# Attention scores and weighted values in two halves each, q's projection as a block of its own, and masks of 32 rows, in a six-layer windowed-attention kernel

## The chip, the core and the metric

The kernel runs on one core of one Trainium2 chip. The metric is device time in microseconds (us) for one execution of the whole program, and of several runs the median. The profile is that of one further execution, so its numbers add up to that execution's own time.

## The reference, cut to what matters

The input has 8 sequences of 512 tokens with 128 features. A first block of attention without a softmax (`_L0_attn_ref`) is followed by six layers of windowed attention and feed-forward. The change concerns the six layers' attention alone. Cut down, with 16 heads of 64 features and windows of 32 tokens, it is:

```python
def attn_layer(x, Wqkv, qs, ksc, Wo):
    q, k, v = jnp.split(x @ Wqkv, 3, -1)          # then split into 16 heads of 64
    q = l2norm(q) * qs;  k = l2norm(k) * ksc      # unit length, scales
    q = q * cos * scale + rotate_half(q) * sin * scale
    k = k * cos / scale + rotate_half(k) * sin / scale
    ...
    # each window of 32 queries sees the window before it and its own: 64 keys
    mask = (it < jb) | (it > jb + w) | (jb == -1)
    sim = jnp.where(mask, -big, jnp.einsum('bhwie,bhwje->bhwij', bq, bk2) * 8.0)
    out = jnp.einsum('bhwij,bhwje->bhwie', softmax(sim), bv2)
    return out @ Wo

for i in range(6):
    x = attn_layer(shift_tokens(x), ...) + x
    x = ffn_layer(shift_tokens(x), ...) + x       # layer norm, 128 -> 2 x 341, gelu, 341 -> 128
```

All of it is in fp32.

## The kernel before, in words

**Units.** The first attention block takes the first part of the program (its lines are L187 to L366). Then comes one long loop over `t` (L703). A *unit* is one layer, one sequence and one block of 128 tokens: 6 x 8 x 4 = 192 units. The loop is a software pipeline, written by hand: in slot `t` the helper `at(t, lag, step)` calls each step for unit `t - lag`, so that a unit is projected in slot `t`, transposed and scored in the next, weighted in the one after, and so on.

**The order of work.** PE's order is the order of the source, since the loop stands in `manual_schedule(engines={PE})` (L694). The order on the other engines is made by a scheduler at build time from priorities; `tc.high_priority()` lifts the copies out of PSUM. Once built, every engine's order is fixed, and engines wait for each other by semaphores.

**A slot before the change**, in PE's order: q's projection (`proj`, L421: 2 products of 512 columns, each of which is 2 MATMUL records[...]), the out-projection of unit t-3 (L603), k's projection, the transposes of the exponentials of unit t-2 (`by_keys`), v's projection (`values`, L481), eight transposes of q and k of unit t-1 (`by_features(0)`: heads 0 to 7, four for q, four for k), the weighted values of unit t-2 (`weigh_values`, L574: 64 small products, 128 MATMUL records), eight more transposes (`by_features(4)`), a piece of the feed-forward part, the mask (L527) and scores (L534, again 128 records) of unit t-1, and eight transposes of unit t-2's result (`out_by_features`). All transposes have the helper's line, L70.

The feed-forward part is spread over four slots, so that each slot holds one piece of it: normalization (transposes into `nx`), transposes of the normalized values (`xn`), three pairs of products with a gelu (L625, L626, L628; these slots also switch ACT's function table and back), and the last product (L657).

**What follows on the other engines.** ACT copies each group of four transposes out of PSUM (L514 for qT and kT, L564 for pT, L596 for oT), squares q and k out of PSUM (L444), copies v (L482), and takes 16 exponentials per unit (L546), which need the maximum that DVE takes over all scores (L542). DVE multiplies q and k by the rotary tables (L429, L436) and divides the weighted values (L582). POOL adds the rotary parts and scales to unit length (L454, L470). SP issues the DMAs that lay v out by windows (L489 to L492).

**PSUM**[...] the ring `mm` (2 buffers of 2 banks: q, k, v and feed-forward products), the ring `tr` (2 buffers of 1 bank: every group of four transposes and the out-projection) and `s` (1 buffer of 2 banks: the scores and, in turn, the weighted values). A group of transposes can start when the group before the last has been copied out; v's projection can start when q's PSUM buffer has been read by DVE and ACT.

**The mask** is added by PE: an identity of 128 rows times the mask, once for each half of the heads, into the bank in which the scores then accumulate.

Of the kernel before, what the change touches and what calls it, by code (L numbers as in the profile page):

```python
# [8 lines left out]
F32 = mybir.dt.float32  # L9
BF16 = mybir.dt.bfloat16  # L10
# [16 lines left out]
def sandwich_kernel(ctx: ExitStack, tc: tile.TileContext, ins: dict, out: bass.AP):  # L27
# [37 lines left out]

    mask = const.tile([P, 2 * W], BF16, tag="mask", name="mask")
    mask0 = const.tile([P, 2 * W], BF16, tag="mask0", name="mask0")

    def transposed(ps, src, rows, cols):
        nc.tensor.transpose(ps[:cols, :rows], src, ident[:rows, :rows])  # L70
# [335 lines left out]

        return dict(wqkv=wqkv, wo=wo, w1=w1, w2=w2, tab=tab)

    def proj(u, s):

        L, b, j = u["L"], u["b"], u["j"]
        wqkv, tab = L["wqkv"], L["tab"]
        lhs = state[b][:, j * P : (j + 1) * P]
        if s == 0:
            u["ss"] = f2.tile([P, 2, H], F32, tag="ss", name="ss")
            u["qk"] = f2.tile([P, 2, H, 2, HF], F32, tag="qk", name="qk")
        ss, qk = u["ss"], u["qk"]

        ps = psum.tile([P, 2, H, HF], F32, tag="mm", name="mm")
        for a in range(2):  # L420
            nc.tensor.matmul(  # L421
                ps[:, a].rearrange("p h d -> p (h d)"), lhs, wqkv[:, s, a, :], start=True, stop=True
            )
        sq = f2.tile([P, H, 2, HF], F32, tag="sq", name="sq")
        t1 = f2.tile([P, 2, H, HF], F32, tag="t1", name="t1")
        t2 = f2.tile([P, 2, H, HF], F32, tag="t2", name="t2")

        def turned(a):
            nc.vector.tensor_tensor(  # L429
                t2[:, a], ps[:, 1 - a],  # L430
                tab[:, 2 * s + 1, j, HF * a : HF * (a + 1)].unsqueeze(1).to_broadcast([P, H, HF]),
                ALU.mult,
            )

        def straight():
            nc.vector.tensor_tensor(  # L436
                t1, ps,
                tab[:, 2 * s, j, :].rearrange("p (a d) -> p a d", a=2).unsqueeze(2)
                .to_broadcast([P, 2, H, HF]),
                ALU.mult,  # L440
            )

        def squared(a):
            nc.scalar.activation(sq[:, :, a, :], ps[:, a], AF.Square)  # L444

        turned(0)
        turned(1)
        straight()
        squared(0)
        squared(1)  # L450
        u["sq"] = sq
        if s == 0:
            sum_squares(u, 0)
        nc.gpsimd.tensor_tensor(qk[:, s].rearrange("p h a d -> p a h d"), t1, t2, ALU.add)  # L454
# [17 lines left out]
            )  # L472

    def values(u):
        L, b, j = u["L"], u["b"], u["j"]
        lhs = state[b][:, j * P : (j + 1) * P]

        v0 = f3.tile([P, 2, 512], F32, tag="v0", name="v0")
        ps = psum.tile([P, 2, 512], F32, tag="mm", name="mm")
        for p in range(2):  # L480
            nc.tensor.matmul(ps[:, p, :], lhs, L["wqkv"][:, 2, p, :], start=True, stop=True)  # L481
        nc.scalar.copy(v0, ps)  # L482

        v2 = f2.tile([P, 4, 512], F32, tag="v2", name="v2")
        for p in range(2):
            if j == 0:
                nc.gpsimd.memset(v2[HD * p : HD * p + W, 0, :], 0.0)
            else:
                nc.sync.dma_start(v2[HD * p : HD * p + W, 0, :], u["B"]["v0"][P - W : P, p, :])  # L489
            nc.sync.dma_start(v2[HD * p + W : HD * (p + 1), 0, :], v0[0:W, p, :])  # L490
            for w in range(1, 4):
                nc.sync.dma_start(  # L492
                    v2[HD * p : HD * (p + 1), w, :], v0[W * (w - 1) : W * (w + 1), p, :]
                )
        u["B"]["v0"] = v0
        u["v2"] = v2

    def by_features(u, c):

        j, qk, B_ = u["j"], u["qk"], u["B"]  # L500
        if c == 0:
            u["qT"] = f1.tile([P, NP, P], F32, tag="qT", name="qT")
            if j == 0:
                B_["kT"] = f2.tile([P, NP, W + P], F32, tag="kT", name="kT")
                nc.gpsimd.memset(B_["kT"][:, :, :W], 0.0)
            u["kT"] = B_["kT"]
        for s in range(2):
            ps = psum.tile([P, 4, P], F32, tag="tr", name="tr")
            for i in range(4):
                h0 = 2 * (c + i)  # L510
                transposed(ps[:, i, :], qk[:, s, h0 : h0 + 2].rearrange("p h a d -> p (h a d)"), P, P)
            dst = u["qT"][:, c : c + 4, :] if s == 0 else u["kT"][:, c : c + 4, W:]
            with tc.high_priority():
                nc.scalar.copy(dst, ps)  # L514
        if c == NP - 4 and j < NB - 1:
            B_["kT"] = f2.tile([P, NP, W + P], F32, tag="kT", name="kT")
            nc.gpsimd.tensor_copy(B_["kT"][:, :, :W], u["kT"][:, :, P:])

    def scores(u):

        qT, kT = u["qT"], u["kT"]


        mk = mask0 if u["j"] == 0 else mask
        sp = psum.tile([P, 2, NP, 2 * W], F32, tag="s", name="sp", bufs=1)
        for p in range(2):
            nc.tensor.matmul(  # L527
                sp[:, p], identb, mk.unsqueeze(1).to_broadcast([P, NP, 2 * W]),
                start=True, stop=False, skip_group_check=True,
            )  # L530
        for pair in range(NP):
            for w in range(4):
                for p in range(2):
                    nc.tensor.matmul(  # L534
                        sp[W * w : W * (w + 1), p, pair, :],
                        qT[HD * p : HD * (p + 1), pair, W * w : W * (w + 1)],
                        kT[HD * p : HD * (p + 1), pair, W * w : W * (w + 2)],
                        start=False, stop=True, skip_group_check=True,
                    )
        mx = f2.tile([P, 2, NP], F32, tag="mx", name="mx")  # L540
        with tc.high_priority():
            nc.vector.tensor_reduce(mx, sp, AX.X, ALU.max, negate=True)  # L542
        pe = f2.tile([P, NP, 2, 2 * W], F32, tag="pe", name="pe")
        for pair in range(NP):
            for p in range(2):
                ex = nc.scalar.activation(  # L546
                    pe[:, pair, p, :], sp[:, p, pair, :], AF.Exp, bias=mx[:, p, pair : pair + 1]
                )
# [14 lines left out]
            with tc.high_priority():  # L563
                nc.scalar.copy(pT[:, c : c + 4, :], ps)  # L564

    def weigh_values(u):

        v2, pT, su = u["v2"], u["pT"], u["su"]
        po = psum.tile([P, 2, NP, HD], F32, tag="s", name="po", bufs=1)
        for pair in range(NP):  # L570
            for w in range(4):
                for p in range(2):
                    r = slice(HD * p, HD * (p + 1))
                    nc.tensor.matmul(  # L574
                        po[W * w : W * (w + 1), p, pair, :],
                        pT[r, pair, W * w : W * (w + 1)],
                        v2[r, w, HD * pair : HD * (pair + 1)],
                        start=True, stop=True,
                    )
        u["on"] = on = f1.tile([P, NP, 2, HD], F32, tag="on", name="on")  # L580
        with tc.high_priority():
            dv = nc.vector.tensor_tensor(  # L582
                on.rearrange("t c p d -> t p c d"), po,
                su.rearrange("t c p -> t p c").unsqueeze(3).to_broadcast([P, 2, NP, HD]), ALU.mult,
            )
        divisions.append(dv)
# [107 lines left out]
    with tc.manual_schedule(engines={mybir.EngineType.PE}):  # L694
# [8 lines left out]
        for t in range(len(units) + 7):  # L703
# [7 lines left out]
            gelus = 0 <= t - 5 < len(units) and units[t - 5]["j"] == NB - 1  # L711
            if gelus:
                gelu_only()
            at(t, 0, proj, 0)
            at(t, 3, out_project)
            at(t, 0, proj, 1)
            at(t, 2, by_keys)

            if t == 0:
                head_norm(NG - 1)  # L720
            at(t, 0, values)
            if t == 1:
                attn_out(B - 1)
            if t == 3:
                to_state(B - 1)
            at(t, 1, by_features, 0)
            at(t, 2, weigh_values)
            at(t, 0, sum_squares, 1)
            if not gelus:
                at(t, 0, unit_length)  # L730
            at(t, 1, by_features, 4)
            at(t, 3, feed_norm, ends=True)
            at(t, 4, feed_first, ends=True)
            at(t, 5, feed_middle, ends=True)
            if gelus:
                at(t, 0, unit_length)
            at(t, 6, feed_last, ends=True)
            at(t, 1, scores)
            at(t, 2, out_by_features)


def _rotary(n):
# [88 lines left out]
```

## Time and profile before

| what | us |
|---|---|
| runs: median of 3 (lowest, highest) | 3899.76 (3896.29, 3900.25) |
| the profiled execution, its own time | 3893.85 |
| span of its profile, first to last instruction | 3892.1 |
| PE busy (matmuls) | 3729.8 |
| DVE busy | 2818.2 |
| ACT busy | 2657.5 |
| POOL busy | 1837.0 |
| matmuls of q's and k's projection, L421 | 727.1 |
| matmuls of v's projection, L481 | 367.9 |
| matmuls of the scores, L534, and of the masks, L527 | 312.2 and 114.6 |
| matmuls of the weighted values, L574 | 299.3 |
| 16 exponentials per unit on ACT, L546 | 651.4 |

How to read the profile: a row of the timeline gives the start (us from the span's start), the time taken, the engine, the line, the operation, the tile written and the tiles read, the shapes, and the number of like instructions merged into the row. In brackets behind it stands the time for which the engine was idle before it, and what ended that idle time. "PEld" rows are weight loads, which overlap the matmuls. In the groups, the first number behind the bar is the busy time (overlaps counted once), the second the mean time of one instruction in ns. Matmuls are pipelined, so that one in a dense run lasts longer than the distance to the next. The granted TensorE clock was 0.99 of full speed.

### The profile page before, as it was taken

To read this page: it belongs to the slowest core of one execution; us is meant where nothing else is said; L and a number is where in the kernel's file an instruction comes from. 1 tells how busy PE (TensorE), PEld (TensorE's weight loads), DVE (VectorE), ACT (ScalarE), POOL (GpSimd) and SP (SyncE) were. 2 spreads that over 40 slices of the span, in tenths; PEclk is the share of its full clock that TensorE was granted. 3 is DMA by queue.
4 is the path that set the end of the run, shared out by engine and by line. 5 is a ranking of instruction groups with operands and counts; after the bars stand their busy time and mean duration, and the time that the engine had idled before them with its cause. 6 is when DMAs were issued, how large, how long until landed. Compare 5 with 4: busy or idle time off the path is not lost.

```text
span 3892.1 us, 149565 instructions
## 1 busy us (share of the span) xinstructions
PE 3729.8 (96%) x65600; PEld 2474.2 (64%) x65600; DVE 2818.2 (72%) x4300; ACT 2657.5 (68%) x6745; POOL 1837.0 (47%) x1311
## 2 busy tenths in 40 slices
PE   8999989999999999999999999999999999999997
PEld 4555456666666666666666666666666666666665
DVE  4555567777867777777777777777787777777775
ACT  5565656776767777777777677777677777766664
POOL 0000025555555555555555555555555555555552
PEclk9999999999999999999999999999999999999998
DMA  2000012222222222222222322223222222222221
GB/s 81 17 9 12 6 50 71 59 66 60 76 74 63 63 63 66 71 75 65 60 62 64 82 65 66 65 56 82 70 66 59 66 65 56 65 68 68 64 67 37
DMA packets 153208, 233.46 MB, mean 60 GB/s; under 512 B 32622, under 2 KB 53356, under 8 KB 151788
## 3 DMA queue, kind: packets, MB, share of 16 engines
q1 hardware_dynamic: 152556, 223.89, 22.4%
q8 instruction: 517, 8.47, 0.9%
q14 instruction: 135, 1.11, 0.1%
HBM read 24.54 MB, written 4.19 MB: 7 GB/s over the span
## 4 chain that ended last, share of the span: by engine, by line
PE 89%; ACT 5%; issue 3%; DVE 2%; DMA 0%; POOL 0%; POOLq 0%; DVEq 0%; SPq 0%; ACTq 0%
PE tr L70 17%; PE mm L421 17%; PE mm L481 9%; PE py L603 9%; PE sp L534 7%; PE po L574 6%; PE y L282 4%; PE mm L625 3%; PE py L657 3%; PE mm L626 3%; PE sc L252 2%; PE sp L527 2%; ACT sq L444 2%; PE vv L230 2%; PE po L318 2%
## 5 line engine op out<-in xcount | busy, mean ns | idle before, releaser
L454 POOL TENSOR_TENSOR qk<-t,t 128x1024 f32<-128x1024 f32 x384 | 909.2, 2368 | 999.6 <-DVE t L436 999.5
L421 PE MATMUL mm<-wqkv,state 128*128 128x512 f32 x1536 | 727.1, 596 | 3.7 <-ACT v L482 2.6
L470 POOL TENSOR_TENSOR qk<-qk,ss 128x1024 f32<-128x1024 f32 x384 | 722.3, 1902 | 16.0
L429 DVE TENSOR_TENSOR t<-mm,tab 128x512 f32<-128x512 f32 x768 | 497.8, 685 | 242.8 <-PE mm L421 231.3
L546 ACT ACTIVATE pe<-sp,mx 128x64 f32<-128x64 f32 x3072 | 651.4, 376 | 27.6 <-DVE mx L542 27.3
L436 DVE TENSOR_TENSOR t<-mm,tab 128x1024 f32<-128x1024 f32 x384 | 465.9, 1213 | 0.0
L457 DVE TENSOR_REDUCE ss<-sq 128x16 f32<-128x1024 f32 x384 | 461.9, 1203 | 2.0 <-ACT sq L444 2.0
L444 ACT ACTIVATE sq<-mm 128x512 f32<-128x512 f32 x768 | 422.6, 610 | 47.2 <-DVE t L436 45.6
L603 PEld LDWEIGHTS py<-oT,wo 128*128 128x128 f32 x3072 | 374.8, 193 | 93.5 <-issue 56.2
L70 PEld LDWEIGHTS tr<-ident,qk 128*128 128x128 f32 x3072 | 345.7, 141 | 127.1 <-issue 105.7
L70 PE MATMUL tr<-ident,qk 128*128 128x128 f32 x3072 | 412.1, 277 | 7.4 <-ACT qT L514 2.3
L596 ACT COPY oT<-tr 128x512 f32<-128x512 f32 x384 | 207.3, 589 | 266.2 <-PE tr L70 265.2
L421 PEld LDWEIGHTS mm<-wqkv,state 128*128 128x128 f32 x1536 | 264.1, 192 | 191.6 <-issue 188.0
L481 PE MATMUL mm<-wqkv,state 128*128 128x512 f32 x768 | 367.9, 602 | 16.8 <-ACT sq L444 16.8
L603 PE MATMUL py<-oT,wo 128*128 128x128 f32 x3072 | 376.0, 276 | 1.0 <-ACT oT L596 0.9
L582 DVE TENSOR_TENSOR on<-po,su 128x1024 f32<-128x1024 f32 x192 | 235.1, 1224 | 170.1 <-PE po L574 170.1
L534 PEld LDWEIGHTS sp<-kT,qT 64*32 64x32 f32 x24576 | 271.9, 106 | 116.7 <-issue 113.8
L574 PE MATMUL po<-v,pT 64*32 64x64 f32 x24576 | 299.3, 225 | 44.7 <-issue 44.7
L482 ACT COPY v<-mm 128x1024 f32<-128x1024 f32 x192 | 194.5, 1013 | 211.0 <-PE mm L481 211.0
L534 PE MATMUL sp<-kT,qT 64*32 64x64 f32 x24576 | 312.2, 227 | 26.0 <-issue 25.2
L574 PEld LDWEIGHTS po<-v,pT 64*32 64x32 f32 x24576 | 258.5, 105 | 86.4 <-issue 86.2
L542 DVE TENSOR_REDUCE mx<-sp 128x16 f32<-128x1024 f32 x192 | 234.6, 1222 | 106.9 <-PE sp L534 106.3
(108 smaller groups left out, 5171.0 us busy)
## 6 DMA issues: line engine op xcount, KB each, us to landing
v<-v SPq DMA_DIRECT2D x1152, 128.0 KB
v<-v SPq DMA_DIRECT2D x672, 64.0 KB
wqkv<-in_L_ffn_Wqkv_dram SPq DMA_DIRECT2D x6, 1536.0 KB
wo<-in_L_ffn_Wo_dram SPq DMA_DIRECT2D x6, 512.0 KB
xin<-_attn_hidden_states_dram SPq DMA_DIRECT2D x8, 256.0 KB
xr<-_attn_hidden_states_dram SPq DMA_DIRECT2D x8, 256.0 KB
x<-xr SPq DMA_DIRECT2D x8, 256.0 KB
xr<-x SPq DMA_DIRECT2D x8, 256.0 KB
```

The source lines that it names most:

```text
L70: nc.tensor.transpose(ps[:cols, :rows], src, ident[:rows, :rows])
L421: nc.tensor.matmul(ps[:, a].rearrange("p h d -> p (h d)"), lhs, wqkv[:, s, a, :], start=True, stop=True)
L429: nc.vector.tensor_tensor(t2[:, a], ps[:, 1 - a], tab[:, 2 * s + 1, j, HF * a : HF * (a + 1)].unsqueeze(1).to_broadcast([P, H, HF]), ALU.mult,
L436: nc.vector.tensor_tensor(t1, ps, tab[:, 2 * s, j, :].rearrange("p (a d) -> p a d", a=2).unsqueeze(2) .to_broadcast([P, 2, H, HF]), ALU.mult,)
L444: nc.scalar.activation(sq[:, :, a, :], ps[:, a], AF.Square)
L454: nc.gpsimd.tensor_tensor(qk[:, s].rearrange("p h a d -> p a h d"), t1, t2, ALU.add)
L470: nc.gpsimd.tensor_tensor(t, t, ss[:, i, :].unsqueeze(2).to_broadcast([P, H, HD]), ALU.mult)
L481: nc.tensor.matmul(ps[:, p, :], lhs, L["wqkv"][:, 2, p, :], start=True, stop=True)
L534: nc.tensor.matmul(sp[W * w : W * (w + 1), p, pair, :], qT[HD * p : HD * (p + 1), pair, W * w : W * (w + 1)], kT[HD * p : HD * (p + 1), pa ...
L546: ex = nc.scalar.activation(pe[:, pair, p, :], sp[:, p, pair, :], AF.Exp, bias=mx[:, p, pair : pair + 1])
L574: nc.tensor.matmul(po[W * w : W * (w + 1), p, pair, :], pT[r, pair, W * w : W * (w + 1)], v2[r, w, HD * pair : HD * (pair + 1)], start=Tru ...
L603: nc.tensor.matmul(py, L["wo"][:, c, :], oT[:, c, :], start=(c == 0), stop=(c == NP - 1))
```

## The change

Six things are changed; the products and sums that are computed stay the same.

1. `proj` is cut into `project(u, s, half)`, one product of 512 columns, and `turn(u, s)`, which holds all that follows q's and k's product on the other engines. v's projection goes through `project` too, and its halves are placed one by one.
2. `weigh_values` runs in two halves of four head pairs each (64 MATMUL records). The first stands between the two halves of v's projection. The division stands on its own (`divide`), behind the second half.
3. `by_features(u, c, s)` makes four transposes at a time, for q (s = 0) or k (s = 1). The first four stand ahead of the second half of the weighted values, and the other twelve behind it.
4. The scores run in two halves. The transposes of `out_by_features` stand between them, and the maximum and exponentials (`softmax`) behind the second half. So the next slot's q projection follows directly on the scores.
5. The mask's left operand is cut to 32 rows: `each` holds four copies of a 32 x 32 identity side by side, on partitions 0 to 31 for the first half of the heads and 32 to 63 for the second. Units with j = 0 (one in four) keep the 128-row identity and `mask0`.
6. `attn_out(B - 1)` of the first attention block moves from slot 1 to the end of slot 0.

The diff, cut to its core:

```diff
+    each = const.tile([2 * W, P], BF16, tag="each", name="each")
+    for a in range(2):
+        for w in range(4):
+            nc.vector.tensor_copy(
+                each[W * a : W * (a + 1), W * w : W * (w + 1)], ident[W * a : W * (a + 1), W * a : W * (a + 1)]
+            )
...
-    def proj(u, s):
+    def project(u, s, half):
+        lhs = state[u["b"]][:, u["j"] * P : (u["j"] + 1) * P]
+        if half == 0:
+            u["proj", s] = psum.tile([P, 2, 512], F32, tag="mm", name="mm")
+        nc.tensor.matmul(
+            u["proj", s][:, half, :], lhs, u["L"]["wqkv"][:, s, half, :], start=True, stop=True
+        )
+    def turn(u, s):
...
-        ps = psum.tile([P, 2, 512], F32, tag="mm", name="mm")
-        for p in range(2):
-            nc.tensor.matmul(ps[:, p, :], lhs, L["wqkv"][:, 2, p, :], start=True, stop=True)
-        nc.scalar.copy(v0, ps)
+        nc.scalar.copy(v0, u.pop(("proj", 2)))
...
-        for s in range(2):
-            ps = psum.tile([P, 4, P], F32, tag="tr", name="tr")
-            for i in range(4):
+        ps = psum.tile([P, 4, P], F32, tag="tr", name="tr")
+        for i in range(4):
...
-    def scores(u):
+    def scores(u, half):
-        mk = mask0 if u["j"] == 0 else mask
-        sp = psum.tile([P, 2, NP, 2 * W], F32, tag="s", name="sp", bufs=1)
-        for p in range(2):
+        if half == 0:
+            u["sp"] = psum.tile([P, 2, NP, 2 * W], F32, tag="s", name="sp", bufs=1)
+        sp = u["sp"]
+        for p in range(2) if half == 0 else ():
+            r = slice(W * p, W * (p + 1))
+            lhs, mk = (identb, mask0) if u["j"] == 0 else (each[r], mask[r])
             nc.tensor.matmul(
-                sp[:, p], identb, mk.unsqueeze(1).to_broadcast([P, NP, 2 * W]),
+                sp[:, p], lhs, mk.unsqueeze(1).to_broadcast([lhs.shape[0], NP, 2 * W]),
                 start=True, stop=False, skip_group_check=True,
             )
-        for pair in range(NP):
+        for pair in range(NP // 2 * half, NP // 2 * (half + 1)):
...
-    def weigh_values(u):
+    def weigh_values(u, half):
-        for pair in range(NP):
+        for pair in range(NP // 2 * half, NP // 2 * (half + 1)):
...
-            at(t, 0, proj, 0)
+            at(t, 0, project, 0, 0)
+            at(t, 0, project, 0, 1)
+            at(t, 0, turn, 0)
             at(t, 3, out_project)
-            at(t, 0, proj, 1)
+            at(t, 0, project, 1, 0)
+            at(t, 0, project, 1, 1)
+            at(t, 0, turn, 1)
             at(t, 2, by_keys)
...
+            at(t, 0, project, 2, 0)
+            at(t, 2, weigh_values, 0)
+            at(t, 0, project, 2, 1)
             at(t, 0, values)
-            if t == 1:
-                attn_out(B - 1)
             if t == 3:
                 to_state(B - 1)
-            at(t, 1, by_features, 0)
-            at(t, 2, weigh_values)
+            at(t, 1, by_features, 0, 0)
+            at(t, 2, weigh_values, 1)
+            at(t, 2, divide)
+            at(t, 1, by_features, 0, 1)
             at(t, 0, sum_squares, 1)
...
-            at(t, 1, by_features, 4)
+            at(t, 1, by_features, 4, 0)
+            at(t, 1, by_features, 4, 1)
...
             at(t, 6, feed_last, ends=True)
-            at(t, 1, scores)
+            if t == 0:
+                attn_out(B - 1)
+            at(t, 1, scores, 0)
             at(t, 2, out_by_features)
+            at(t, 1, scores, 1)
+            at(t, 1, softmax)
```

In the changed kernel's lines the projections are all L421, the weighted values L590, the masks L538, the scores L545, the squares L455, the copies of qT and kT L521, that of v L489, and the transposes L77.

More of the change, by code (lines that the diff above doesn't have):

```diff
@@ L407, in load_layer @@
         return dict(wqkv=wqkv, wo=wo, w1=w1, w2=w2, tab=tab)
-    def proj(u, s):
+    def project(u, s, half):
[6 more added lines that the diff above has]
+    def turn(u, s):
         L, b, j = u["L"], u["b"], u["j"]
-        wqkv, tab = L["wqkv"], L["tab"]
-        lhs = state[b][:, j * P : (j + 1) * P]
+        tab = L["tab"]
         if s == 0:
@@ L417, in proj @@
         ss, qk = u["ss"], u["qk"]
[L419 to L423, printed above, removed]
+        ps = u.pop(("proj", s)).rearrange("p a (h d) -> p a h d", d=HF)
         sq = f2.tile([P, H, 2, HF], F32, tag="sq", name="sq")
@@ L474, in values @@
     def values(u):
-        L, b, j = u["L"], u["b"], u["j"]
-        lhs = state[b][:, j * P : (j + 1) * P]
+        j = u["j"]
         v0 = f3.tile([P, 2, 512], F32, tag="v0", name="v0")
-        ps = psum.tile([P, 2, 512], F32, tag="mm", name="mm")
-        for p in range(2):
-            nc.tensor.matmul(ps[:, p, :], lhs, L["wqkv"][:, 2, p, :], start=True, stop=True)
-        nc.scalar.copy(v0, ps)
+        nc.scalar.copy(v0, u.pop(("proj", 2)))
         v2 = f2.tile([P, 4, 512], F32, tag="v2", name="v2")
@@ L496, in values, with by_features @@
         u["v2"] = v2
-    def by_features(u, c):
+    def by_features(u, c, s):
         j, qk, B_ = u["j"], u["qk"], u["B"]
-        if c == 0:
+        if c == 0 and s == 0:
             u["qT"] = f1.tile([P, NP, P], F32, tag="qT", name="qT")
+        if c == 0 and s == 1:
             if j == 0:
@@ L506, in by_features @@
             u["kT"] = B_["kT"]
-        for s in range(2):
-            ps = psum.tile([P, 4, P], F32, tag="tr", name="tr")
-            for i in range(4):
[L510 to L515, printed above, removed]
+        ps = psum.tile([P, 4, P], F32, tag="tr", name="tr")
+        for i in range(4):
+            h0 = 2 * (c + i)
+            transposed(ps[:, i, :], qk[:, s, h0 : h0 + 2].rearrange("p h a d -> p (h a d)"), P, P)
+        dst = u["qT"][:, c : c + 4, :] if s == 0 else u["kT"][:, c : c + 4, W:]
+        with tc.high_priority():
+            nc.scalar.copy(dst, ps)
+        if c == NP - 4 and s == 1 and j < NB - 1:
             B_["kT"] = f2.tile([P, NP, W + P], F32, tag="kT", name="kT")
             nc.gpsimd.tensor_copy(B_["kT"][:, :, :W], u["kT"][:, :, P:])
-    def scores(u):
+    def scores(u, half):
         qT, kT = u["qT"], u["kT"]
-        mk = mask0 if u["j"] == 0 else mask
-        sp = psum.tile([P, 2, NP, 2 * W], F32, tag="s", name="sp", bufs=1)
-        for p in range(2):
+        if half == 0:
[4 more added lines that the diff above has]
+            lhs, mk = (identb, mask0) if u["j"] == 0 else (each[r], mask[r])
             nc.tensor.matmul(
-                sp[:, p], identb, mk.unsqueeze(1).to_broadcast([P, NP, 2 * W]),
+                sp[:, p], lhs, mk.unsqueeze(1).to_broadcast([lhs.shape[0], NP, 2 * W]),
                 start=True, stop=False, skip_group_check=True,
             )
-        for pair in range(NP):
+        for pair in range(NP // 2 * half, NP // 2 * (half + 1)):
             for w in range(4):
@@ L539, in scores, with softmax @@
                     )
+    def softmax(u):
+        sp = u.pop("sp")
         mx = f2.tile([P, 2, NP], F32, tag="mx", name="mx")
@@ L564, in by_keys @@
                 nc.scalar.copy(pT[:, c : c + 4, :], ps)
-    def weigh_values(u):
-        v2, pT, su = u["v2"], u["pT"], u["su"]
-        po = psum.tile([P, 2, NP, HD], F32, tag="s", name="po", bufs=1)
-        for pair in range(NP):
+    def weigh_values(u, half):
+        v2, pT = u["v2"], u["pT"]
+        if half == 0:
+            u["po"] = psum.tile([P, 2, NP, HD], F32, tag="s", name="po", bufs=1)
+        for pair in range(NP // 2 * half, NP // 2 * (half + 1)):
             for w in range(4):
@@ L574, in weigh_values @@
                     nc.tensor.matmul(
-                        po[W * w : W * (w + 1), p, pair, :],
+                        u["po"][W * w : W * (w + 1), p, pair, :],
                         pT[r, pair, W * w : W * (w + 1)],
@@ L579, in weigh_values, with divide @@
                     )
+    def divide(u):
+        po, su = u.pop("po"), u["su"]
         u["on"] = on = f1.tile([P, NP, 2, HD], F32, tag="on", name="on")
```

## The prediction

> **What bounds the kernel now.** I read the page first (busy shares, DMA queues, the chain that ended last), then the timeline of one pass of the loop over `t` ("a unit", of which there are 192), then the waits.
>
> ```profile
> PE 3729.8 (96%) x65600; PEld 2474.2 (64%) x65600; DVE 2818.2 (72%) x4300; ACT 2657.5 (68%) x6745; POOL 1837.0 (47%) x1311
> ...
> q8 instruction: 517, 8.47, 0.9%
> ...
> PE 89%; ACT 5%; issue 3%; DVE 2%; DMA 0%; POOL 0%; POOLq 0%; DVEq 0%; SPq 0%; ACTq 0%
> ```
>
> PE is busy 96% and holds 89% of the chain, so time is won or lost on PE. ACT, at 68%, looks far from the limit. One unit of the timeline shows how PE and ACT are laced:
>
> ```profile
> 2014.52 1.88 PE L421 MATMUL mm<-wqkv,state 128*128 128x512 f32 x4
> ...
> 2015.55 3.38 ACT L546 ACTIVATE pe<-sp,mx 128x64 f32<-128x64 f32 x16 [0.19 <-DVE mx L542]
> ...
> 2019.02 1.08 ACT L444 ACTIVATE sq<-mm 128x512 f32<-128x512 f32 x2
> ...
> 2020.61 1.88 PE L481 MATMUL mm<-wqkv,state 128*128 128x512 f32 x4
> ...
> 2022.33 1.04 PE L70 MATMUL tr<-ident,qk 128*128 128x128 f32 x8
> ...
> 2022.53 1.01 ACT L482 COPY v<-mm 128x1024 f32<-128x1024 f32 x1 [1.08 <-PE mm L481]
> ...
> 2023.30 1.48 PE L574 MATMUL po<-v,pT 64*32 64x64 f32 x128
> 2023.44 0.59 ACT L514 COPY qT<-tr 128x512 f32<-128x512 f32 x1
> 2023.92 0.61 ACT L514 COPY kT<-tr 128x512 f32<-128x512 f32 x1
> 2024.45 1.08 ACT L444 ACTIVATE sq<-mm 128x512 f32<-128x512 f32 x2
> ...
> 2024.71 1.09 PE L70 MATMUL tr<-ident,qk 128*128 128x128 f32 x8
> ...
> 2025.42 0.59 ACT L514 COPY qT<-tr 128x512 f32<-128x512 f32 x1
> ...
> 2025.89 0.61 ACT L514 COPY kT<-tr 128x512 f32<-128x512 f32 x1
> ...
> 2026.06 0.66 PE L70 MATMUL tr<-ident,xn 128*128 128x128 f32 x4 [0.25 <-ACT qT L514]
> ...
> 2026.56 0.59 PE L527 MATMUL sp<-mask,identb 128*128 128x512 bf16 x2
> ...
> 2027.08 1.82 PE L534 MATMUL sp<-kT,qT 64*32 64x64 f32 x128
> ```
>
> See that a PE row begins where the one before it leaves off, and that ACT works through copies just in time: the xn transposes already wait for a qT copy. The two bursts of 128 small matmuls (L574, L534) can stall, as in the next unit, which also holds the three gelus:
>
> ```profile
> 2033.89 1.28 ACT L82 ACT_TABLE_LOAD   x1
> ...
> 2035.19 1.09 ACT L444 ACTIVATE sq<-mm 128x512 f32<-128x512 f32 x2
> ...
> 2036.33 1.98 PE L481 MATMUL mm<-wqkv,state 128*128 128x512 f32 x4 [0.31 <-ACT sq L444]
> ...
> 2041.49 0.43 PE L574 MATMUL po<-v,pT 64*32 64x64 f32 x24 [1.09 <-issue]
> ```
>
> "Issue" there means that nothing in the profile held PE. Counting PE's records in the trace, 86 of the 87 such stalls over 0.4 us stand at the same place modulo 256 instructions, and the page's q8 line is 517 packets of 16.4 KB[...] (65600 + 65600 records make 513 such blocks). So they are waits for the next block of instructions. Without a stall a burst takes 1.413 us from the end of the group before to its own end. All L574 bursts together take 329.0 us against 191 x 1.413 = 269.9, all L534 bursts 324.8 against 192 x 1.414 = 271.5: **59 + 53 = 112 us** is stall.
>
> [...] L252, which has 32 rows, has 1024 x 481 ns = 493 us of matmuls in 106.0 us of busy time.
>
> **Prices.** A switch into a burst: transposes start at 2022.33, eight take 0.87, the burst starts at 2023.30: 0.10. Half a burst: in the records of a burst without a stall the 64th matmul starts 0.61 after the first and the next group 0.15 after the last one: 0.76, so two halves take 1.51 against 1.41 whole. The group behind a burst is slower by 0.06 (transposes, 0.93 against 0.87) or 0.10 (512 columns). A further switch out and back costs 0.10 + 0.10 + 0.06 to 0.10, **about 0.28 us**.
>
> **The change, part by part.** (1) *Two more bursts a unit*: 2 x 0.28 x 189 = +104 us, all on PE. (2) *The block stalls*: in the trace's packet records a stall ends 2.2 to 2.9 us after its block's packet began. A whole burst with little ahead of it leaves less; two halves with what lies between them take 0.76 + 0.96 + 0.54 + 0.76 = 3.0 for the weighted values and 0.76 + 1.03 + 0.76 = 2.6 for the scores, before which PE is slow. I take all 112 us as gone; bounds 0 and -112. (3) *Masks of 32 rows* in three units of four: two matmuls side by side save 0.21, one more mode (0.10) comes in: -0.11 x 141 = -16 us. Bounds -30 and +14[...]. (4) *q's projection behind, transposes regrouped, copies*: here the cost lies. A cast of `each` (eight small copies) and `attn_out` in the slot before touch the start alone; I take nothing, at most 5 us either way.
>
> The program's order on ACT, which the build fixes, changes. Before, a unit has v, qT, kT, sq (of k), qT, kT. After, 142 units have v, qT, **sq, kT**, qT, kT. And PE now does the first four q transposes, half the weighted values, and then *twelve* transposes in a row (k, q, k) through the two `tr` buffers, so that the third group waits for the copy of the first one (kT), which stands behind sq, behind qT, behind the copy of v. And v is finished later, since half a burst lies inside it.
>
> Worked out on a clock that starts at the unit's first q matmul (2014.52 above). PE: q 1.82 (1.72, and 0.10 behind a burst), out-projection 1.79, k 1.72, eight transposes 0.87: 6.20. Half of v 0.86, switch 0.10, half burst 0.76, other half of v 0.86 + 0.10: 8.88. Four transposes 0.44, switch 0.10, half burst 0.76: 10.18. k's four 0.50, q's four 0.44: the third group could start at **11.12**. ACT: v's copy starts 0.20 behind PE's next group (2022.33 to 2022.53), 9.08; qT 0.91 later, 9.99; sq 0.51 later, 10.50 (its DVE products were done by 9.9: sq started at 9.93 before); kT 0.97 later (2024.45 to 2025.42), 11.47, and it takes 0.61: 12.08. PE goes on at **12.13**: a wait of 1.01. What is queued behind it on PE: the feed-forward piece, masks, scores, and so the next unit. From there: transposes 0.44, the piece's four 0.44, switch and masks 0.42, half burst 0.76, transposes 0.93, switch 0.10, half burst 0.76: the next unit starts at 15.98.
>
> Periods of before from the trace (mean from one unit's first q matmul to the next's): 15.08 with nx in it (47), 15.91 with xn (46), 20.23 with the gelus (46), 16.99 with the last product (40; the 6 with the final norm go along). After: nx 15.98, +0.90. The xn unit's scores wait 0.31 for the last kT copy (13.43 against 13.12), and its exps start some 0.25 later, because four xn products now precede the maximum on DVE: 16.54, +0.63. The last product: 15.98 - 0.44 + 2.58 = 18.12, +1.13.
>
> The gelu unit has another order on ACT: table load, then **both pT copies, then sq**. Scores now end right before q, so exps run from 1.5 to 4.89, the table to 6.18, pT to 7.16, sq to 8.25: v's first half, which needs q's PSUM buffer, starts at 8.30 instead of 6.20. A wait of 2.10 (0.47 before), and everything on PE behind it. The later wait then vanishes, since ACT's sq of k is done early: 15.98 - 1.01 + 2.10 - 0.44 + 5.20 = 21.83, +1.60.
>
> **Sum**: 47 x 0.90 + 46 x 0.63 + 46 x 1.13 + 46 x 1.60 = 42 + 29 + 52 + 74 = **+197 us**. By parts: switches +104, masks -16, stalls -112, kT wait 1.01 x 142 = +143, xn +26, gelu (2.10 - 0.47) x 46 = +75, xn's old wait for qT, about 22, gone: +198. The profiled execution took 3893.85 (span 3892.1); 4091 for it. The median of the runs shown is 5.9 higher: **4097**.
>
> **Rivals.** *A, PE alone counts* (the other side): if copies are off the path as ACT's 68% suggests, what is left is +104 - 16 - 112 - 22 = -46: 3854, faster. It decides if the first kT copy is done by 11.12, 1.0 us sooner than I get, and if the gelu unit's sq needs no more than it did. Against it: the order on ACT is fixed, each link of the chain has its duration above, and DVE's and PE's parts of it cannot start sooner. *B, stalls stay in the halves of the scores*: [...] +53: 4150. For it: a block's stall can last over a microsecond. *C, switches cost half*[...]: -52: 4045. Against it: 0.10 in and 0.06 out are seen in every unit.
>
> **Chances.** Main case 0.62 (4055 to 4140), B 0.15, C 0.12, A 0.08, between them at no change 0.03. What a measurement of this kernel can tell from no change is about 0.2%. Faster 0.08, same 0.03, slower 0.89. The range leaves out A and takes in C with the masks' and stalls' bounds below, and B above: 3990 to 4165.
>
> **What would show it.** In the new profile PE's transposes of qk should show about 140 us of idle before them, put down to ACT kT L521; the projection's matmuls L421 about 95 us put down to ACT sq L455; L590 and L545 almost no issue idle over 0.4 us; what follows a half burst starting 0.76 us after it; mask pairs starting together. If qk transposes do not wait for kT, I am wrong and A holds. If stalls of 0.5 us or more remain in L545, B holds.

## The result, and the profile after

The changed kernel takes **4154.46 us** (median of 4 runs, 4147.08 to 4159.44), the kernel before, on the same chip, 3898.03: a ratio of **1.0658**, 95% interval 1.0635 to 1.0681. That is 256 us slower; predicted were 197 over the median shown, with a range that ends at 4165. The profiled execution spans 4148.2 us, at a granted clock of 0.988. Of all runs in this document one of e3's twelve fell in a slow state (7337.43 us), and its ratio leaves that run out.

The page of the changed kernel, its busy times, the q8 queue, and the chain that ended last:

```profile
span 4148.2 us, 149528 instructions
...
PE 3867.4 (93%) x65600; PEld 2463.1 (59%) x65600; DVE 2843.5 (69%) x4308; ACT 2659.5 (64%) x6745; POOL 1844.9 (44%) x1311
...
q8 instruction: 517, 8.47, 0.9%
...
PE 82%; ACT 15%; DVE 1%; issue 1%; DMA 0%; POOL 0%; POOLq 0%; ACTq 0%; DVEq 0%; SPq 0%
```

ACT is busy for 2 us more than before, and yet its share of the chain goes from 5% to 15%: it has no more work, its work is in the way. "Issue" falls from 3% to 1%, though q8 moves as many packets of instructions, 517. The groups of PE in the kernel before, and those of the changed kernel:

```profile
L421 PE MATMUL mm<-wqkv,state 128*128 128x512 f32 x1536 | 727.1, 596 | 3.7 <-ACT v L482 2.6 <-issue 1.0
L70 PE MATMUL tr<-ident,qk 128*128 128x128 f32 x3072 | 412.1, 277 | 7.4 <-ACT qT L514 2.3 <-issue 2.2 <-ACT pT L564 1.2
...
L481 PE MATMUL mm<-wqkv,state 128*128 128x512 f32 x768 | 367.9, 602 | 16.8 <-ACT sq L444 16.8
L534 PE MATMUL sp<-kT,qT 64*32 64x64 f32 x24576 | 312.2, 227 | 26.0 <-issue 25.2
L574 PE MATMUL po<-v,pT 64*32 64x64 f32 x24576 | 299.3, 225 | 44.7 <-issue 44.7
```

```profile
L421 PE MATMUL mm<-wqkv,state 128*128 128x512 f32 x2304 | 1175.5, 620 | 91.2 <-ACT sq L455 91.2
L77 PE MATMUL tr<-ident,qk 128*128 128x128 f32 x3072 | 456.5, 282 | 126.2 <-ACT kT L521 122.4 <-ACT qT L521 2.5 <-DVE state L348 0.7
...
L590 PE MATMUL po<-v,pT 64*32 64x64 f32 x24576 | 338.7, 227 | 3.9 <-issue 3.1
L545 PE MATMUL sp<-kT,qT 64*32 64x64 f32 x24576 | 336.8, 225 | 6.8 <-issue 6.6
```

Behind the second bar stands PE's idle time ahead of each group. Matmuls overlap: L421's 1536 of 596 ns before are 915 us, in 727.1 us of busy time. The two new waits are there: 122.4 us for the kT copy ahead of the transposes, and 91.2 us for the squares ahead of the projection (16.8 before). The issue idle of the bursts is almost gone (44.7 and 25.2 before). PE and ACT rows from the timeline of one xn unit, in which the first wait arises:

```profile
2207.75 1.02 PE L421 MATMUL mm<-wqkv,state 128*128 128x512 f32 x2
...
2208.71 0.86 PE L590 MATMUL po<-v,pT 64*32 64x64 f32 x64
...
2209.50 1.12 PE L421 MATMUL mm<-wqkv,state 128*128 128x512 f32 x2
...
2210.66 1.01 ACT L489 COPY v<-mm 128x1024 f32<-128x1024 f32 x1 [2.07 <-PE mm L421]
...
2211.57 0.59 ACT L521 COPY qT<-tr 128x512 f32<-128x512 f32 x1
...
2211.78 1.09 PE L77 MATMUL tr<-ident,qk 128*128 128x128 f32 x8
...
2212.04 1.11 ACT L455 ACTIVATE sq<-mm 128x512 f32<-128x512 f32 x2
...
2213.01 0.62 ACT L521 COPY kT<-tr 128x512 f32<-128x512 f32 x1
...
2213.68 0.66 PE L77 MATMUL tr<-ident,qk 128*128 128x128 f32 x4 [0.81 <-ACT kT L521]
```

The v copy waits for the second half of v, behind the half burst. qT, sq and kT follow it without a gap. The last four transposes start when the kT copy ends, 0.81 us after PE was free. In a gelu unit the second wait is seen, and a smaller one for kT:

```profile
2223.33 1.28 ACT L89 ACT_TABLE_LOAD   x1
...
2223.88 1.04 PE L77 MATMUL tr<-ident,pe 128*128 128x128 f32 x8
...
2224.63 1.07 ACT L579 COPY pT<-tr 128x512 f32<-128x512 f32 x2
...
2225.58 1.11 ACT L455 ACTIVATE sq<-mm 128x512 f32<-128x512 f32 x2
...
2226.74 1.13 PE L421 MATMUL mm<-wqkv,state 128*128 128x512 f32 x2 [1.82 <-ACT sq L455]
...
2232.26 0.66 PE L77 MATMUL tr<-ident,qk 128*128 128x128 f32 x4 [0.29 <-ACT kT L521]
```

Table load, pT copies, squares, and only then v's first half.

### The profile page after: what moved, and what is told of

It reads as the page before. It is cut to its first block, busy times and chain, and to the rows that moved or that the text cites. A ratio compares the mean times of both kernels' runs of the same rounds, so it can differ in the third digit from the quotient of the medians.

```text
span 4148.2 us, 149528 instructions
## 1 busy us (share of the span) xinstructions
PE 3867.4 (93%) x65600; PEld 2463.1 (59%) x65600; DVE 2843.5 (69%) x4308; ACT 2659.5 (64%) x6745; POOL 1844.9 (44%) x1311
## 4 chain that ended last, share of the span: by engine, by line
PE 82%; ACT 15%; DVE 1%; issue 1%; DMA 0%; POOL 0%; POOLq 0%; ACTq 0%; DVEq 0%; SPq 0%
PE mm L421 25%; PE tr L77 14%; PE py L623 8%; PE sp L545 7%; PE po L590 5%; ACT sq L455 4%; PE y L289 4%; ACT v L489 3%; PE mm L645 3%; PE py L677 3%; PE mm L646 3%; ACT kT L521 2%; PE sc L259 2%; ACT qT L521 2%; PE sp L538 2%; PE vv L237 2%
## 5 line engine op out<-in xcount | busy, mean ns | idle before, releaser
L421 PE MATMUL mm<-wqkv,state 128*128 128x512 f32 x2304 | 1175.5, 620 | 91.2 <-ACT sq L455 91.2
L421 PEld LDWEIGHTS mm<-wqkv,state 128*128 128x128 f32 x2304 | 380.7, 192 | 327.8 <-issue 190.6
L77 PE MATMUL tr<-ident,qk 128*128 128x128 f32 x3072 | 456.5, 282 | 126.2 <-ACT kT L521 122.4
L77 PEld LDWEIGHTS tr<-ident,qk 128*128 128x128 f32 x3072 | 343.4, 142 | 299.6 <-ACT kT L521 167.5
L447 DVE TENSOR_TENSOR t<-mm,tab 128x1024 f32<-128x1024 f32 x384 | 465.7, 1213 | 0.0
L455 ACT ACTIVATE sq<-mm 128x512 f32<-128x512 f32 x768 | 429.0, 627 | 45.0 <-DVE t L447 44.8
L489 ACT COPY v<-mm 128x1024 f32<-128x1024 f32 x192 | 194.3, 1012 | 368.7 <-PE mm L421 368.7
L590 PEld LDWEIGHTS po<-v,pT 64*32 64x32 f32 x24576 | 271.9, 106 | 187.5 <-ACT pT L579 108.4
L545 PE MATMUL sp<-kT,qT 64*32 64x64 f32 x24576 | 336.8, 225 | 6.8 <-issue 6.6
L590 PE MATMUL po<-v,pT 64*32 64x64 f32 x24576 | 338.7, 227 | 3.9 <-issue 3.1
L545 PEld LDWEIGHTS sp<-kT,qT 64*32 64x32 f32 x24576 | 273.2, 106 | 93.5 <-issue 93.5
L521 ACT COPY kT<-tr 128x512 f32<-128x512 f32 x384 | 229.6, 598 | 73.4 <-PE tr L77 72.0
```

Source lines behind the costliest of these rows:

```text
L421: nc.tensor.matmul(u["proj", s][:, half, :], lhs, u["L"]["wqkv"][:, s, half, :], start=True, stop=True)
L447: nc.vector.tensor_tensor(t1, ps, tab[:, 2 * s, j, :].rearrange("p (a d) -> p a d", a=2).unsqueeze(2) .to_broadcast([P, 2, H, HF]), ALU.mult,)
L545: nc.tensor.matmul(sp[W * w : W * (w + 1), p, pair, :], qT[HD * p : HD * (p + 1), pair, W * w : W * (w + 1)], kT[HD * p : HD * (p + 1), pa ...
L590: nc.tensor.matmul(u["po"][W * w : W * (w + 1), p, pair, :], pT[r, pair, W * w : W * (w + 1)], v2[r, w, HD * pair : HD * (pair + 1)], star ...
```

## The experiments

Two theories. **T**: most of the loss is the fixed order of ScalarE (ACT), which puts the squares of k ahead of the kT copy, with twelve transposes behind it, and in gelu units the pT copies ahead of the squares of q. **R**: the two added bursts of TensorE (PE) and their switches are the loss, and ScalarE's waits only show slack. Times, each with the kernel before on the same chip:

| run | us | before | ratio and interval |
|---|---|---|---|
| e1_scores_whole | 4044.61 | 3893.05 | 1.0390 (1.0374 to 1.0405) |
| e2_values_whole | 4020.55 | 3893.05 | 1.0323 (1.0305 to 1.0341) |
| e3_both_whole | 3896.36 | 3893.05 | 1.0005 (0.9995 to 1.0014) |
| e4_v_first | 4143.64 | 3893.05 | 1.0645 (1.0626 to 1.0664) |
| e5_values_spread | 3915.77 | 3893.11 | 1.0057 (1.0043 to 1.0071) |
| e6_gelu_squares_first | 4106.33 | 3893.11 | 1.0553 (1.0537 to 1.0569) |
| e7_no_k_squares | 4069.94 | 3893.11 | 1.0451 (1.0437 to 1.0465) |
| e8_masks_alone | 3884.80 | 3893.11 | 0.9976 (0.9967 to 0.9985) |
| e9_both_split_spread | 4004.13 | 3896.45 | 1.0277 (1.0263 to 1.0291) |
| e10_masks_table_later | 3887.32 | 3896.45 | 0.9978 (0.9969 to 0.9986) |
| e11_values_close | 3870.67 | 3888.29 | 0.9957 (0.9943 to 0.9971) |

The trace also gives the mean time from one unit's first q matmul to the next one's, by the feed-forward piece in it. This separates better than the totals:

| us | nx (47) | xn (46) | gelu (46) | last (40) |
|---|---|---|---|---|
| before | 15.08 | 15.91 | 20.23 | 16.99 |
| changed kernel | 16.16 | 16.30 | 22.88 | 18.37 |
| e1_scores_whole | 15.92 | 16.26 | 21.14 | 18.14 |
| e2_values_whole | 15.16 | 16.52 | 21.83 | 17.25 |
| e3_both_whole | 15.18 | 15.84 | 20.12 | 16.98 |
| e6_gelu_squares_first | 16.17 | 16.32 | 21.82 | 18.37 |
| e7_no_k_squares | 15.52 | 15.98 | 22.83 | 17.92 |

**One part of the change at a time.** e1 puts the scores back into one burst, e2 the values, e3 both. The edit of e1, and that of e2:

```diff
             at(t, 1, scores, 0)
-            at(t, 2, out_by_features)
             at(t, 1, scores, 1)
             at(t, 1, softmax)
+            at(t, 2, out_by_features)
```

```diff
             at(t, 0, project, 2, 0)
-            at(t, 2, weigh_values, 0)
             at(t, 0, project, 2, 1)
             at(t, 0, values)
...
             at(t, 1, by_features, 0, 0)
+            at(t, 1, by_features, 0, 1)
+            at(t, 2, weigh_values, 0)
             at(t, 2, weigh_values, 1)
             at(t, 2, divide)
-            at(t, 1, by_features, 0, 1)
```

> The changed kernel with its scores in one burst again (both halves, then the softmax, then the transposes of the output); values stay in halves, masks of 32 rows. Theory T (ScalarE's order): the twelve transposes in a row stay, and with them the order v, qT, squares of k, kT; so units with an nx, xn or last piece keep what they lost in the changed kernel (about +130 us in all), gelu units lose about 1.0 us each like them instead of 2.65 (+46), since their ScalarE order becomes squares ahead of the two pT copies again: 4075 us, and L77 still waits over 120 us for kT. Rival R (the added bursts and their switches are the loss, evenly for each split step): half of the loss of 256 us goes: 4026 us.

> The changed kernel with v's projection whole, eight transposes, and the weighted values in one burst behind them; scores stay in halves, masks of 32 rows. T: ScalarE's order in 142 units is that of the kernel before (v, qT, kT, squares of k), so nx, xn and last units come within 0.2 us of the kernel before (15.1, 15.9 and 17.0 us); only the 46 gelu units lose, about 2.4 us each, since there the two pT copies stand ahead of the squares of q: before + 110 - 16 for the masks = 3990 us. R: half of the loss goes, evenly over all kinds of units: 4026 us, with nx at 15.6.

> The changed kernel with both split steps whole again, so that the masks of 32 rows (and attn_out of the last sequence one unit earlier) are what is left of the change. T and R alike: 0.11 us less for each of 141 units, 16 us: 3882 us; the stalls inside the bursts of scores and values are back at 25 and 45 us.

Over e3 the split of the values costs 148 us (e1) and that of the scores 124 us (e2), together 272; the whole change cost 258 over e3 (4154.46 - 3896.36, on two chips). So the two parts nearly add. By totals alone R's 4026 is nearer to both (19 and 5 us off) than T's figures (30 us off each). What separates is where the time goes. The two largest waits of e1's transposes and projection, from its waits:

```profile
PE tr L77 <- ACT kT L521: 140.0, 191, 0.8
PE mm L421 <- ACT sq L455: 20.8, 47, 5.2
```

and of e2:

```profile
PE mm L421 <- ACT sq L455: 99.4, 83, 5.2
...
PE tr L77 <- ACT qT L521: 17.4, 48, 2.5
```

(us in all, how often, the longest.) Each part owns one wait: the values the wait for kT, the scores that for the squares. e2's nx units take what e3's do (15.16 and 15.18 us), though they have the additional burst. R expected +0.5 there. T's sizes were off by 30 us either way. e1 is lower, in the main because 0.24 us of what nx and last units lost in the changed kernel goes with its scores (16.16 to 15.92, 18.37 to 18.14). e2 is higher: its maximum comes behind the layer norm on DVE, so in xn units the exponentials start at 2.29 us of the unit instead of 1.33, and v's matmuls wait for the squares there too (83 waits instead of e3's 47).

e3 was a miss for both: the masks gained nothing in it. Summed from the end of each PE step to the end of the next, mask pairs take 16.6 us less than before, the scores behind them 8.4 more and the moved attn_out 4.4 more. e8 below takes this up.

**v ahead of the first half burst.**

```diff
             at(t, 0, project, 2, 0)
-            at(t, 2, weigh_values, 0)
             at(t, 0, project, 2, 1)
             at(t, 0, values)
+            at(t, 2, weigh_values, 0)
```

> The changed kernel with v's two half projections together ahead of the first half of the values; all four half bursts stay, and the twelve transposes too. T: v's copy on ScalarE comes about 1 us earlier, so that the kT copy is limited by its own transposes and the third group of transposes waits 0.35 us instead of 0.81: -65 us (-50 to -90), about 4090 us; gelu units as they are. R: as many bursts, switches and transposes as in the changed kernel: 4154 us.

A miss for T: 4143.64, not 4090. The v copy did come 1 us earlier, but its lead was lost one place on. The timeline of an xn unit of e4, ACT and PE rows:

```profile
2208.68 1.01 ACT L489 COPY v<-mm 128x1024 f32<-128x1024 f32 x1 [1.08 <-PE mm L421]
...
2209.36 0.66 PE L77 MATMUL tr<-ident,qk 128*128 128x128 f32 x4
...
2210.59 0.60 ACT L455 ACTIVATE sq<-mm 128x512 f32<-128x512 f32 x1 [0.90 <-DVE t L447]
...
2211.08 0.58 ACT L521 COPY qT<-tr 128x512 f32<-128x512 f32 x1
...
2211.72 0.66 PE L77 MATMUL tr<-ident,qk 128*128 128x128 f32 x4 [0.33 <-ACT qT L521]
...
2212.70 0.66 PE L77 MATMUL tr<-ident,qk 128*128 128x128 f32 x4 [0.33 <-ACT kT L521]
```

The order is now v, sq, qT, sq, kT. The square waits 0.90 us until DVE has read the same PSUM tile (L447), and qT, whose transposes ended at 2210.02, starts at 2211.08, behind it on ACT. In the waits, kT falls from 122.4 to 60.1 us and qT rises from 2.5 to 42.3. So the late v copy alone is not what costs. The place of the squares of k is the next thing to test.

**Without the squares of k, and with the pT copies behind the squares of q.** e7 leaves out the two squares of k. e6 holds pT behind the squares (`q_squares` collects the second square of q of each unit) and qT behind v, where it was:

```diff
-        squared(0)
-        squared(1)
-        u["sq"] = sq
+        if s == 0:
+            squared(0)
+            squared(1)
+            u["sq"] = sq
```

```diff
             with tc.high_priority():
-                nc.scalar.copy(pT[:, c : c + 4, :], ps)
+                cp = nc.scalar.copy(pT[:, c : c + 4, :], ps)
+            issue_behind(cp, q_squares[-1])
```

> The changed kernel with ScalarE's two pT copies behind the squares of q in all units, as in the kernel before, which moves them in the 46 gelu units alone (and the qT copy held behind the v copy, as it was). T: the squares end at 7.1 us of a gelu unit instead of 8.1, v's first half starts as much earlier and nothing else is late: 46 x 0.95 = -44 us, 4110 us; L421's wait for the squares falls from 91 us to about 47. R: as many bursts and switches: 4154 us.

> The changed kernel without ScalarE's squares of k: k is normed by the sums of q's squares, so that part of the computation is left out; VectorE's sums and all of TensorE's work stay. T: the kT copy follows the qT copy at once, the third group of the twelve transposes hardly waits: 0.65 us less in 142 units and 0.3 us in 46, -105 us, 4050 us (4030 to 4080), and L77's wait for kT falls from 122 us to under 40. R: TensorE's work is the same: 4154 us.

e6 gives 4106.33 against 4110 expected. The gelu unit goes from 22.88 to 21.82 and no other kind moves by over 0.02: 46 x 1.06 = 49 us, and the span of its profile is 48.3 us below that of the changed kernel. L421 of e6 and L77 of e7:

```profile
PE mm L421 <- ACT sq L455: 44.7, 48, 5.2
```

```profile
PE tr L77 <- ACT kT L522: 53.9, 190, 0.6
```

In e7 the span falls by 80.6 us (4148.2 to 4067.6), and it is the nx, xn and last units that fall, by 0.64, 0.32 and 0.45; gelu units do not. So what stands ahead of a copy or a square in ScalarE's order is shown to cost about 130 us (49 and 81) without one TensorE instruction taken away, and R alone falls. e6 changes the order and nothing else. e7 takes the squares of k away, and no run only moves them in the changed kernel; but 75 of its 81 us are in the steps of the transposes of q and k (538.1 us in the changed kernel, 463.2 in e7), and L421's wait for the squares of q stays as it was (91.3). T's 105 was too much: 53.9 us of wait stay, 0.28 each time. They belong to the twelve transposes themselves. With two `tr` buffers, the third group can start only when the first one's copy of 0.6 us is done, and only the four transposes of the second group (0.44 us) lie between.

**The half bursts without the twelve transposes in a row.** e5 spreads the values' halves over the sixteen transposes, with the scores whole. e9 does the same with all four half bursts, and with e6's edit.

```diff
             at(t, 0, project, 2, 0)
-            at(t, 2, weigh_values, 0)
             at(t, 0, project, 2, 1)
             at(t, 0, values)
...
             at(t, 1, by_features, 0, 0)
+            at(t, 1, by_features, 0, 1)
+            at(t, 2, weigh_values, 0)
+            at(t, 1, by_features, 4, 0)
             at(t, 2, weigh_values, 1)
             at(t, 2, divide)
-            at(t, 1, by_features, 0, 1)
+            at(t, 1, by_features, 4, 1)
             at(t, 0, sum_squares, 1)
...
-            at(t, 1, by_features, 4, 0)
-            at(t, 1, by_features, 4, 1)
```

> Values still in two half bursts, but v's projection whole, and the sixteen transposes of q and k as eight, half burst, four, half burst, four, so that no twelve stand in a row; scores in one burst, masks of 32 rows. ScalarE's order is that of the kernel before. It has as many bursts and transposes as e1_scores_whole. T: against e3_both_whole one more burst, +0.36 x 190 = +68 us by the tail-to-tail steps, less about 39 us of issue stalls in the values' bursts: 3925 us (3890 to 3950), and the transposes' wait for kT is gone. R (a burst more costs what e1 showed, wherever it stands): 4045 us.

> All four half bursts of the changed kernel and the masks of 32 rows, but ScalarE's order of the kernel before in every unit: v whole and the sixteen transposes spread as in e5_values_spread, and the pT copies behind the squares of q in gelu units as in e6_gelu_squares_first. T: e5_values_spread, plus what the split scores cost apart from the order in gelu units (e2_values_whole less e3_both_whole, 124 us, less the 1.0 us x 46 that e6_gelu_squares_first took back): 3916 + 78 = 3994 us (3970 to 4015); what is left against the kernel before is the later exponentials and the switches. R (the bursts and switches themselves): as the changed kernel, 4154 us.

e5 has e1's bursts and transposes and is 129 us faster (3915.77 where T expected 3925, e1 4044.61). Its wait for kT is gone, and the burst is paid for by stalls that went; what is left is a new wait, for the division:

```profile
PE sp L545 <- issue: 23.7, 25, 3.3
PE mm L421 <- ACT sq L455: 19.5, 45, 5.2
PE sp L538 <- DVE on L602: 19.4, 60, 0.7
...
PE po L590 <- issue: 5.3, 14, 1.0
```

Scores and weighted values share one PSUM buffer, so the masks wait until DVE has read the values, which now end four transposes later: 19.4 us in 60 waits.

e9 gives 4004.13, inside T's 3970 to 4015. With the changed kernel's four half bursts, 150 of its 256 us are gone. R as stated is out. Step by step on PE, e9 is 85 us above e5: 78 in L421 (37 from q's projection starting behind a burst, 0.195 x 190, and most of the rest from 35 us more waiting for the squares) and 17 in the transposes of pe, less some in the bursts. L421's wait in e9 (19.5 in e5, above):

```profile
PE mm L421 <- ACT sq L455: 55.1, 93, 5.2
```

So splitting the scores has a price of its own, which the orders tried here do not cure: the exponentials, and all behind them on ACT, come later. They start at 1.37 us of an nx unit instead of 0.72 in e5, and at 2.48 of an xn unit instead of 1.75.

**Masks alone, and a version that is faster.** e8 is the kernel before with the masks of 32 rows and nothing else. e10 adds to it the gelu table behind the squares of q:

```diff
-            if gelus:
-                gelu_only()
             at(t, 0, proj, 0)
+            if gelus:
+                gelu_only()
...
         issue_behind(ld, exps[-1])
+        issue_behind(ld, q_squares[-1])
```

> The kernel before with the masks of 32 rows alone. If what e3_both_whole gave back (0.11 us less for each of 144 pairs of masks, but 8 us more in the bursts of scores behind them and 4 us more in the last attn_out) is tied to the masks in its first part and to the moved attn_out in its second: -16.6 + 8 = 3885 us, ratio 0.998. If the 8 us came from where the blocks of instructions happen to lie: anywhere from 3876 to 3900 us.

> e8_masks_alone with the gelu table loaded behind the squares of q instead of ahead of them: in gelu units ScalarE runs exponentials, squares, table, pT copies. T: the squares end 0.9 us earlier there, v's matmuls follow them up to the end of the transposes of pe, 0.35 to 0.45 us earlier, in 46 units: -16 to -20 us, 3866 us; L488's wait for the squares falls from 16 us to next to nothing. Rival: the pT copies, 1.3 us behind the squares, become what the values' burst waits for, and nothing is gained: 3885 us.

e8 gives 3884.80, the 3885 expected: masks pay 0.24%. Mask pairs take 16.8 us less and the scores behind them 6.6 more. e10 gives 0.9978, nothing gained over e8, though not as the rival said. The wait was removed as planned (16.2 to 3.6 us). A gelu unit of e10 shows what took it back:

```profile
2029.39 1.88 PE L429 MATMUL mm<-wqkv,state 128*128 128x512 f32 x4
...
2035.49 1.88 PE L490 MATMUL mm<-wqkv,state 128*128 128x512 f32 x4
...
2037.21 1.04 PE L77 MATMUL tr<-ident,qk 128*128 128x128 f32 x8
...
2038.17 1.28 PE L584 MATMUL po<-v,pT 64*32 64x64 f32 x104
...
2041.61 0.43 PE L584 MATMUL po<-v,pT 64*32 64x64 f32 x24 [2.15 <-issue]
```

The same unit of the kernel before, whose v projection starts at 2036.33:

```profile
2029.76 1.88 PE L421 MATMUL mm<-wqkv,state 128*128 128x512 f32 x4
...
2039.11 1.28 PE L574 MATMUL po<-v,pT 64*32 64x64 f32 x104
2041.49 0.43 PE L574 MATMUL po<-v,pT 64*32 64x64 f32 x24 [1.09 <-issue]
```

Counted from the unit's first q matmul (2029.39 and 2029.76), v's projection starts 0.47 us earlier than before and the burst 0.57, and yet the burst, which stops behind its 104th matmul in both, goes on 0.49 us later, after 2.15 us instead of 1.09. Not every unit is like it: on average over the 46 gelu units, the burst starts 0.59 us earlier than in e8 and ends 0.17 us earlier, and the unit takes 20.20 us against 20.16. The issue idle of this line in the whole kernel is 42.5 us in e8 and 67.2 in e10:

```profile
L582 PE MATMUL po<-v,pT 64*32 64x64 f32 x24576 | 299.5, 226 | 42.5 <-issue 42.5
```

```profile
L584 PE MATMUL po<-v,pT 64*32 64x64 f32 x24576 | 299.5, 225 | 67.2 <-issue 67.2
```

The profiled execution of e10 took 3895.02 us, 8 us above the median of its runs, so a usual run may add less than these 25 us.

This pointed to half bursts after all, placed so that nothing else moves. e11 is e10 with the values in halves, four transposes between them, and the squares of k held behind the kT copy:

```diff
             at(t, 1, by_features, 0, 0)
+            at(t, 2, weigh_values, 0)
             at(t, 1, by_features, 0, 1)
-            at(t, 2, weigh_values, 0)
+            if t < len(units):
+                units[t].pop("square")(kT_copies[-1:])
             at(t, 2, weigh_values, 1)
             at(t, 2, divide)
```

(The lines with a minus are those of the values whole, as in e2; `square` issues the squares of k, behind the kT copy given.)

> e10_masks_table_later with the weighted values in two half bursts: v whole, four transposes, half burst, four transposes, half burst, eight transposes; the squares of k held behind the kT copy, so that ScalarE's order stays that of the kernel before. No twelve transposes stand in a row, and the second half burst is 0.4 us later than in one burst, not a unit's middle later as in e5_values_spread. T: an added burst costs what e5_values_spread leaves when its other terms are taken off (+19 measured, +40 and +7 for stalls that went, -19 for the new wait for VectorE's division): 47 us; it takes about 59 of the 67 us of issue stalls out of the values' bursts of e10_masks_table_later: 3887 + 47 - 59 = 3875 us (3860 to 3890). Rival: four transposes between the halves leave too little room for ScalarE's copies, and the third group waits again, 0.3 us in each unit: 3930 us.

e11 gives 3870.67 where T expected 3875, a ratio of **0.9957** (0.9943 to 0.9971), the fastest of all. Its bursts:

```profile
L600 PE MATMUL po<-v,pT 64*32 64x64 f32 x24576 | 337.4, 224 | 19.4 <-issue 18.6
L555 PE MATMUL sp<-kT,qT 64*32 64x64 f32 x24576 | 310.1, 227 | 14.7 <-issue 13.8
```

Here the split that cost 148 us in e1 pays: 0.9978 becomes 0.9957, 8 us by the ratios, with intervals that overlap at their ends (0.9969 and 0.9971).

## Why the prediction was right, and which sizes were off

The direction and the mechanism held: both waits arose where the prediction put them (122.4 us for kT, about 140 forecast; 91.2 for the squares, about 95), and e6 and e7 show that they are causes. The sum came out 58 us too small (198 by parts, 256 measured). So 4154 lies above the main case (4055 to 4140), and inside the range only because the range was drawn to take in rival B, whose 4150 is nearest by the total. That nearness is chance: most of the stalls that B kept are gone, as its term below shows, and other terms made up the sum.

From the steps of PE's trace, end to end, and the periods:

- **Switches, +104 predicted.** Mis-sized. From end to end a half burst takes 0.788 us, so two take 0.16 more than a whole one (1.413), and a matmul of 512 columns behind a burst ends 0.195 later than behind transposes (1.914 against 1.719). That makes 0.36 for an added burst, not 0.28; 2 x 0.36 x 189 = +136. I had read the exit from starts alone.
- **Stalls, -112 predicted.** Near. By the same reckoning (sum less number times stall-free step) 59 + 53 before, 14 + 15 after: -83. Rival B had kept all 53 in the scores' halves; 15 stayed, with five waits of over 0.5 us where there had been 17.
- **Masks, -16.** The pairs (144, not 141) alone give -17, and e8 shows 6.6 given back in the scores behind them. The two matmuls of a pair start 2 to 5 ns apart, where with 128 rows it was 215 or more. The parts of the 0.11 (0.21 gained, 0.10 lost to a switch) were an estimate.
- **kT wait and xn, +147** (143 + 26 - 22). The transposes of q and k and of xn take 144 us more in the changed kernel. Of this the gelu units have 27 (0.59 each), where I said that the wait vanishes; the others have 117, less than I gave them. That the term is right to 3 us is luck: the two errors cancel. The failing step is "the later wait then vanishes, since ACT's sq of k is done early": the kT copy cannot begin before its transposes end, and twelve in a row keep 0.3 us of idle time with no square in the way (e7; from end to end 0.44 to 0.55 us in its nx, last and gelu units).
- **Gelu, +75.** L421 takes 156 us more; less 2 x 0.195 x 190 = 74 for exits this is 82. Near.

The differences are +32, +29, -1, -3 and +7, together 64; the transposes of `on` take 5 us less, which no step had foreseen, and that makes the 58 within 1. **Per kind** the clock gave 15.98, 16.54, 21.83 and 18.12 us; measured 16.16, 16.30, 22.88 and 18.37. Only gelu is far off: there kT's wait and the exits come together. The argument took it that ScalarE's copies keep their place in the order that the build gives them, even when their transposes are done. e4 agrees: its qT copy above stood for 1.06 us behind a square (2210.02 to 2211.08). So do e6 (another order, 48.3 us off the span) and e7 (no squares of k, 80.6 us).

Rival A (PE alone counts) fell by the waits themselves, C (cheap switches) by the 0.36. What stays open is why a packet of q8 begins when it does. In e10 PE's starting the burst 0.59 us sooner brought its end forward by 0.17 us on average; the cause was not found.

## What to carry to other kernels

Before splitting a step on the busiest engine, write down the order that the copy engine will then have, in each kind of pass, and follow the buffer that the last group waits for: ACT, busy for 64% of the span, cost 48 us by its order alone (e6). Split where the copies keep their order and their room (e11), not where the split leaves twelve transposes in a row that wait for a copy (the changed kernel); putting v together again, as e4 did, gave back next to nothing (1.0645 against 1.0658). And where a dense run of small matmuls stalls on issue, look at that idle time before counting a gain upstream: in e10 it grew from 42.5 to 67.2 us, and nothing was gained.

## What the runs showed of the hardware

- A pair of masks with 32-row operands takes 0.32 us from end to end (changed kernel), one with 128 rows 0.43 to 0.45 (kernel before).
- The stalls in the bursts come to 112 us before, to 148 in the profiled execution of e10, to 69 in e11, where the values are halved, and to 29 in the changed kernel, where both are, all with 49152 matmuls in the bursts: that number alone does not set them.
- PE's records, its sequencer's among them, number 132355 before and 132353 in the changed kernel, within 3 of 517 times 256, and q8 moves 517 packets in both. The six issue stalls over 0.4 us that the changed kernel keeps all fall on one of two neighbouring places modulo 256, the same two as before, and end 2.5 to 3.2 us after a packet of q8 began.
- Behind a burst of small matmuls, eight transposes end 0.15 us later than behind large matmuls (1.024 against 0.874, kernel before), and q's two products of 512 columns 0.195 us later than behind transposes (1.914 in the changed kernel, 1.719 before).
